# Moving the even-bank copy and the odd bank to the end of a turn in a one-core convolution kernel

## The chip, the cores and the metric

The kernel runs on one core of one Trainium2 chip. The time of a run is the device time of that core in microseconds (us). Beside the times there is the profile of one execution, in which each engine's instructions have a start and a length. The engines are TensorE (PE, matrix products), VectorE (DVE), ScalarE (ACT), GpSimd (POOL) and SyncE (SP, which starts transfers). Each works through its own queue in order and waits for others by semaphores.

## The reference

```
x: (160, 128, 32, 32) float32; U: (5, 128*128*9) float32
s1 = (max(U) - min(U)) / 3;  s2 = s1 / 5
v1 = s1 * floor(U / s1);  v2 = s2 * floor((U - v1) / s2)
w  = (v1 + v2) as (5 * 128, 128, 3, 3)
g  = group norm of x (32 groups of 4 channels, eps 1e-5)
image 5*b + n is convolved with weight set n (3 x 3, padding 1)
out = x + conv(g, w)
```

So each of the 160 images of 128 channels and 32 x 32 points is normalised, convolved with one of five quantised weight sets, and added to itself.

## The kernel before

The images are worked through in turns, `i` = 0 to 159, ordered by weight set (32 images for each). Tensors lie with the channels on the 128 partitions; an image is 1024 points in the free dimension. Products are in float16 with the operand split into a high part and a rest, so that the sum is nearly float32.

A convolution over pairs of neighbouring points is done with fewer products. For each image there are two banks of PSUM (128 x 512, float32), the even and the odd outputs. A "direct" image pairs rows: its high part `hi` goes through all nine taps (L784), its rest is combined into `rows` (L760 to L769) for L839. A "combined" image pairs columns: the differences and sums of points are made first (`v`, L674 and L704 on POOL, L686 and L693 on DVE, the last two in `combine`), then split into `vh` (ACT L734) and `vl` (DVE L740), and both go through L839. From image 7 to 29 the odd images are combined and the even ones direct.

Per image, PE, ACT and DVE work together like this:

- `begin` (PE): opens the even bank with the products of the sum quarter, 3 matmuls for a direct image, 6 for a combined one.
- `leave` (ACT L907): copies this even bank to `half` in SBUF.
- `complete` (PE): adds the products of the difference quarter to the even bank, 3 or 6 matmuls; it overwrites what `leave` reads, so it waits for it.
- `odd_from_even` (DVE L914): odd = 2 * half - even; it waits for `complete`.
- `main(i, 0)` and `main(i, 1)` (PE): the products of the even and of the odd bank, 12 matmuls each for a direct image, 6 for a combined one. `main(i, 0)` writes the even bank that L914 reads, so it waits for L914 of its image.
- `residual` (ACT L942): copies both banks to `sum`, which POOL's DMA adds to the output (L963, `accumulate`).

Nothing plans the order: the calls in `run` and `conv` are the order of each queue. The turns stand in three forms. Turn 3 (`FIRST`) has a form of its own. In turns 4 to 27, `conv(i)` gives PE `begin(i+1)`, `main(i, 0)`, `complete(i+1)`, `main(i, 1)`; ACT has `leave(i+1)` as the turn's first instruction. From turn `TWO_AHEAD` = 28 on (`steady`), `begin` runs two images ahead, `complete(i+1)` and `begin(i+2)` come ahead of the main products, and ACT's `leave(i+2)` stands behind the first statistics.

After `conv`, a turn's ACT queue has the sums for the statistics of an image some 10 to 16 turns ahead (L241), the copies of image i-1 (L942), the high part of the image two or three ahead (L734, or L636 and L644) and the squares (L248). The DVE queue has the low parts of the image two ahead (three from turn 13 on: L740, or L747 to L769) with a step of the next weight set (`later.take`, L142 to L162, L544), then L914 for image i+1, then `combine` for the image four ahead (five from turn 11 on) with another step of the weights, and for some images the statistics by DVE (L231 to L235, `BY_VECTOR`). POOL's part of `v` starts after DVE's low part of the turn (`beside_pairs`).

PSUM holds four even banks, three odd banks and a small one. SP loads two images in one DMA and stores them to the output as they are, ahead of the accumulating DMA.

Of the kernel before, what the change touches and what calls it, by code (L numbers as in the profile page):

```python
# [36 lines left out]
class Later:  # L37
# [25 lines left out]
    def finish(self):  # L63
        run(self.steps)
# [110 lines left out]
def last_of(steps, last=None):  # L175
    for last in steps:
        pass
    return last


def run(steps):

    while True:
        try:
            next(steps)
        except StopIteration as end:
            return end.value
# [134 lines left out]
def general_path(tc, keep, steps, x, u, out):  # L322
# [8 lines left out]
    with tc.If(far > 0), ExitStack() as ctx:  # L331
# [9 lines left out]
        for n in range(N_SETS):  # L341
            un = one.tile([P, C, TAPS], F32, tag="u", name=f"g_u{n}")
            nc.sync.dma_start(un, uv[n])
            wn = one.tile([P, C, TAPS], F32, tag="w", name=f"g_w{n}")
            k1, k2 = run(steps.quantise(one, un, f"g{n}", F32))
            nc.vector.tensor_scalar_mul(wn, k1, steps.s1)
            nc.vector.scalar_tensor_tensor(wn, k2, steps.s2, wn, ALU.mult, ALU.add)
# [38 lines left out]
class Main:  # L386
# [23 lines left out]

    STAT_LEAD = 15
    FURTHER = 11
    TWO_AHEAD = 28
    LOAD_LEAD = 18
    CHUNKS = 11
    STEADY = 7
# [174 lines left out]
    def keep_sums(self, n, col):  # L591
        wt = self.wts[n, col]
        run(self.both_sums(
            self.nc.gpsimd, wt[:, self.SUM], wt[:, self.DIFF], *(wt[:, k] for k in range(ROW))
        ))
# [263 lines left out]
    def steady(self, i):  # L859

        return i >= self.TWO_AHEAD

    def conv(self, i, on_the_way):


        ahead = range(i + 1, self.imgs)[:1]
        if self.steady(i) and self.steady(i - 1):
            for k in ahead:
                self.complete(k)
            for k in range(i + 2, self.imgs)[:1]:  # L870
                self.begin(k)
            self.main(i, 0, lambda: on_the_way(self.COLS[1]))
            self.main(i, 1, lambda: on_the_way(self.COLS[2]))
        elif i == self.FIRST:
            self.main(i, 0)
            self.begin(i + 1)
            on_the_way(self.COLS[1])
            self.main(i, 1)
            on_the_way(self.COLS[2])
            self.leave(i + 1)  # L880
            self.complete(i + 1)
        else:
            self.begin(i + 1)
            self.main(i, 0, lambda: on_the_way(self.COLS[1]))
            self.leave(i + 1)
            self.complete(i + 1)
            if self.steady(i):
                self.begin(i + 2)
            self.main(i, 1, lambda: on_the_way(self.COLS[2]))
        del self.v[i]  # L890

# [101 lines left out]
    def run(self):  # L993
# [54 lines left out]
        def measure(stage, *images):  # L1048
            for i in images:
                self.measure(i, (stage,))  # L1050
# [74 lines left out]
        for i in range(self.imgs):  # L1125
# [3 lines left out]
            def on_the_way(col):  # L1129
                if col == self.COLS[1]:  # L1130
                    for st in ready:
                        st.means(self.pg)
                    for *column, parts in self.columns:
                        self.turn_column(*column, parts)
                        turned.append(column)
                    self.columns.clear()
                if col == self.COLS[2]:
                    for st in middle:
                        st.variances()
# [39 lines left out]
            if i < self.FIRST:  # L1179

                if i == 0:
                    measure(0, 8, 9, 10)
                if i == 1:
                    self.normalise(4)
                    self.high_part(4)
                if i == 2:
                    self.normalise(5)
                    measure(1, 9)
                    self.high_part(5)
                    self.odd_from_even(3)  # L1190
                    self.low_part(4)
                    run(self.combinations(4))
                    measure(0, 11)
                self.residual(j)
            else:

                last = None
                for k in self.step_of(i, 2):
                    if self.combined(k):
                        last = last_of(self.low_combined(k), last)  # L1200
                    else:
                        self.low_part(k)
                        later.take(1)
                        last = last_of(self.combinations(k), last)
                last = later.take(1, last)
                if last:
                    before = self.last_but_one(last)
                    for st in scaled:
                        self.after(st.power(), before)
                    for k in self.step_of(i, 4):  # L1210
                        self.beside_pairs(k, before)
                if i > self.FIRST and self.by_hand(j):
                    self.residual(j)
                for k in by_scalar:
                    self.measure(k, (0,))
                if self.steady(i) and i + 2 < self.imgs:
                    self.leave(i + 2)
                if i > self.FIRST and not self.by_hand(j):
                    self.residual(j)
                    self.accumulate(j)  # L1220
                for st in ready:
                    if not st.late:
                        st.deviations()
                for k in self.step_of(i, 3):
                    if self.combined(k):
                        self.high_combined(k)
                        continue
                    if self.by_scalar_too(k):
                        self.normalise(k)
                    self.high_part(k)  # L1230
                for k in by_scalar:
                    self.measure(k, (1,))
# [13 lines left out]

            if i >= self.FIRST:

                if i + 1 < self.imgs:
                    self.odd_from_even(i + 1)  # L1250
                for st in scaled:
                    st.scales_by_vector()
                for k in self.step_of(i, 4):
                    if self.combined(k):
                        self.combine(k)
                    later.take(1)
                later.take_scalar()
                if b in (self.per_set - 4, self.per_set - 2):
                    later.finish()
                for st in ready:  # L1260
                    if st.late:
                        st.deviations_by_vector()
# [65 lines left out]
```

## Time and profile before

| what | value |
|---|---|
| median of 3 runs | 971.14 us (970.75 to 971.58) |
| the profiled execution | 971.98 us, its span 970.2 us |
| PE busy | 928.3 us, 96% of the span, 4432 matmuls |
| DVE busy | 858.9 us, 89% |
| ACT busy | 863.3 us, 89% |
| POOL busy | 446.0 us, 46% |
| mean granted TensorE clock | 0.993 |
| moved by DMA | 254.23 MB, mean 262 GB/s |

A row of instructions gives start, length, engine, line, operation, output from inputs, and, in brackets, how long the engine was idle before it and what ended that. A row of waits gives who waited for whom: total us, times, longest us. A matmul's length is its way through the array (0.38 us); in a row of matmuls one starts every 0.2125 us at the full clock.

### The profile page before, as it was taken

How to read it: one execution, taken by the hardware profiler on the slowest of the kernel's cores; microseconds unless marked ns; L12 is line 12 of the kernel's file. 1: busy time of each engine (PE TensorE's matmuls, PEld its weight loads, DVE VectorE, ACT ScalarE, POOL GpSimd, SP SyncE). 2: the span in 40 equal slices, each digit the busy share in tenths (PEclk: the TensorE clock that was granted, in tenths of full speed). 3: DMA queues.
4: the chain of work that ended last, by engine and by line, in shares of the span. 5: the costliest groups of instructions: out<-in, count | busy, mean ns of one | idle time of the engine just before them, and what ended most of it. 6: DMA issues, size and time to landing. Idle time of an engine off the chain costs nothing.

```text
span 970.2 us, 12948 instructions
## 1 busy us (share of the span) xinstructions
PE 928.3 (96%) x4432; PEld 434.6 (45%) x4432; DVE 858.9 (89%) x1125; ACT 863.3 (89%) x1320; POOL 446.0 (46%) x481
## 2 busy tenths in 40 slices
PE   2899979999999999999999999999999999999996
PEld 1444434444444444444444444444444444444442
DVE  7988878888899899998999899898989988889973
ACT  5779879998999999999999999999999999997660
POOL 4354433544453443454445444545444455454640
PEclk9999989999999999999999999999999999999998
DMA  9079999999999999999999999999999999756554
GB/s 353 29 270 351 329 353 330 328 326 329 321 314 317 259 283 294 276 284 269 290 252 308 286 282 284 289 277 297 263 274 266 290 280 258 162 90 102 95 93 128
DMA packets 67450, 254.23 MB, mean 262 GB/s; under 512 B 5296, under 2 KB 5296, under 8 KB 67376
## 3 DMA queue, kind: packets, MB, share of 16 engines
q1 hardware_dynamic: 45344, 173.09, 47.8%
q0 software_dynamic: 22032, 80.23, 44.1%
q8 instruction: 37, 0.61, 0.2%
q14 instruction: 37, 0.30, 0.1%
HBM read 89.19 MB, written 164.10 MB: 261 GB/s over the span
## 4 chain that ended last, share of the span: by engine, by line
PE 79%; ACT 10%; DVE 5%; issue 3%; DMA 2%; POOL 1%; SPq 0%; DVEq 0%; ACTq 0%; POOLq 0%
PE even L839 43%; PE odd L839 14%; PE even L784 11%; PE odd L784 11%; ACT junk L248 2%; ACT vh L734 2%; ACT sum L942 2%; ACT junk L241 2%; DMA u<-in_L_conv_U_dram 2%; ACT z L636 1%; ACT half L907 1%; ACT hi L644 1%; DVE ext L508 1%; DVE ext L509 1%; DVE lo L747 1%
## 5 line engine op out<-in xcount | busy, mean ns | idle before, releaser
L839 PEld LDWEIGHTS <-wt 128*128 128x128 f16 x1884 | 184.3, 99 | 211.2 <-issue 4.4
L740 DVE SCALAR_TENSOR_TENSOR vl<-v,rstd,vh 128x2048 f16<-128x2048 f32 x94 | 235.2, 2502 | 48.6 <-ACT vh L734 48.4
L839 PE MATMUL even<-vh,across 128*128 128x512 f16 x564 | 211.3, 375 | 3.5 <-ACT half L907 3.5
L839 PE MATMUL even<-vl,across 128*128 128x512 f16 x564 | 211.3, 375 | 1.7 <-DVE vl L740 1.7
L734 ACT ACTIVATE vh<-v,rstd 128x2048 f16<-128x2048 f32 x94 | 190.2, 2024 | 0.0
L784 PEld LDWEIGHTS <-wt 128*128 128x128 f16 x1242 | 121.7, 100 | 144.2 <-issue 6.6
L248 ACT ACTIVATE junk<-xt,mv 128x1024 uint8<-128x1024 f32 x152 | 176.4, 1160 | 0.3
L839 PE MATMUL even<-rows,wt 128*128 128x512 f16 x567 | 174.2, 381 | 2.5 <-ACT half L907 2.4
L963 POOL DMA_DIRECT2D out_dram<-sum x153 | 135.2, 884 | 89.7 <-ACT sum L942 74.5
L241 ACT ACTIVATE junk<-xt 128x1024 uint8<-128x1024 f32 x152 | 161.2, 1060 | 12.7 <-DMA xt<-in_x_dram 9.8
L839 PEld LDWEIGHTS <-across 128*128 128x128 f16 x1128 | 110.4, 98 | 135.5 <-issue 7.5
L784 PE MATMUL even<-hi,wt 128*128 128x496 f16 (+3 forms) x594 | 162.9, 379 | 4.8 <-DVE odd L914 3.8
L710 POOL TENSOR_SCALAR z<-xt,ngm,rstd 128x1024 f32<-128x1024 f32 x49 | 91.8, 1873 | 152.1 <-DVE rows L769 50.5
L784 PE MATMUL odd<-hi,wt 128*128 128x496 f16 (+3 forms) x594 | 161.0, 375 | 0.0
L686 DVE TENSOR_TENSOR v<-xt 128x960 f32<-128x960 f32 x94 | 155.8, 1658 | 0.5 <-POOL v L674 0.5
L907 ACT COPY half<-even 128x512 f32<-128x512 f32 x157 | 90.6, 577 | 60.1 <-PE even L839 57.1
L674 POOL TENSOR_SCALAR v<-xt,ngm 128x64 f32<-128x64 f32 x94 | 59.0, 628 | 172.8 <-DVE vl L740 74.8
L914 DVE SCALAR_TENSOR_TENSOR odd<-half,even 128x512 f32<-128x512 f32 x157 | 107.8, 687 | 17.3 <-PE even L839 13.8
L839 PE MATMUL even<-vh,wt 128*128 128x496 f16 (+1 forms) x282 | 105.6, 375 | 0.0
L839 PE MATMUL even<-vl,wt 128*128 128x496 f16 (+1 forms) x282 | 105.6, 375 | 0.0
L839 PE MATMUL odd<-vl,wt 128*128 128x496 f16 (+1 forms) x282 | 105.6, 374 | 0.0
L839 PE MATMUL odd<-vh,wt 128*128 128x496 f16 (+1 forms) x282 | 105.6, 374 | 0.0
(148 smaller groups left out, 1131.1 us busy)
## 6 DMA issues: line engine op xcount, KB each, us to landing
xt<-in_x_dram SPq DMA_DIRECT2D x78, 1024.0 KB, 9.6
out_dram<-sum POOLq DMA_DIRECT2D x153, 512.0 KB, 8.8
out_dram<-xt SPq DMA_DIRECT2D x76, 1024.0 KB, 14.2
out_dram<-xt SPq DMA_DIRECT2D x7, 512.0 KB, 6.1
u<-in_L_conv_U_dram SPq DMA_DIRECT2D x4, 576.0 KB, 14.7
xt<-in_x_dram SPq DMA_DIRECT2D x4, 512.0 KB, 9.8
range<-in_L_conv_U_dram SPq DMA_DIRECT2D x3, 576.0 KB, 8.0
u<-in_L_conv_U_dram SPq DMA_DIRECT2D x2, 288.0 KB, 3.0
```

What stands on the lines that cost most here:

```text
L241: self.nc.scalar.activation(junk, image, ACTF.Copy, scale=-1.0 / image.shape[1], accum_out=self.mv[:, j, 0:1],)
L248: self.nc.scalar.activation(junk, image, ACTF.Square, bias=self.mv[:, j, 0:1], accum_out=self.mv[:, j, 1:2],)
L674: return self.nc.gpsimd.tensor_scalar(self.view(self.v[i], 0, (512 + W // 2 - 1, 2), (W // 2, H)), self.view(self.image(i), 1, (W - 3, 2), ...
L686: nc.vector.tensor_tensor(self.view(v, 1, (511, 2), (half, H), (1, half - 1)), self.view(x, 1, (1, 2), (W, H), (2, half - 1)), self.view(x ...
L710: ins = nc.gpsimd.tensor_scalar(z, self.image(i), st.ngm[:, j], st.rstd[:, j], ALU.add, ALU.mult)
L734: self.nc.scalar.mul(vh, self.v[i], st.rstd[:, j])
L740: yield self.nc.vector.scalar_tensor_tensor(vl, self.v[i], st.rstd[:, j], self.hi[i], ALU.mult, ALU.subtract)
L784: nc.tensor.matmul(target[a][:, first:end, c0:c1], self.wts[n, col][:, k, :], tile[:, s0 : s0 + 2 * (end - first) - 1 : 2, c0 + dw : c1 + dw],
L839: self.nc.tensor.matmul(out, weights, moving, start=start and j == 0, stop=False, skip_group_check=True)
L907: self.nc.scalar.copy(half, self.eo[i][0])
L914: self.nc.vector.scalar_tensor_tensor(odd, self.half.pop(i), 2.0, even, ALU.mult, ALU.subtract)
L963: added = self.nc.gpsimd.dma_start(self.ov[n, :, b], self.sum.pop(i), accum_op=ALU.add)
```

## The change

In turns 4 up to `TWO_AHEAD`, `leave(i+1)` goes from the start of ACT's turn to behind the copies of image i-1; `complete(i+1)` goes from the middle of PE's turn to its end; and `odd_from_even(i+1)` goes behind `combine` and its step of the weights in DVE's turn. `TWO_AHEAD` becomes 20, so that turns 20 to 27 take the form of the later turns. Turn 3 and turns from 28 on keep their order. Turn 20 is the changeover, as turn 28 was.

```diff
-    TWO_AHEAD = 28
+    TWO_AHEAD = 20
...
             self.leave(i + 1)
             self.complete(i + 1)
-        else:
+        elif self.steady(i):
             self.begin(i + 1)
             self.main(i, 0, lambda: on_the_way(self.COLS[1]))
             self.leave(i + 1)
             self.complete(i + 1)
-            if self.steady(i):
-                self.begin(i + 2)
+            self.begin(i + 2)
+            self.main(i, 1, lambda: on_the_way(self.COLS[2]))
+        else:
+            self.begin(i + 1)
+            self.main(i, 0, lambda: on_the_way(self.COLS[1]))
             self.main(i, 1, lambda: on_the_way(self.COLS[2]))
         del self.v[i]
...
                 if i > self.FIRST and not self.by_hand(j):
                     self.residual(j)
                     self.accumulate(j)
+                if i > self.FIRST and not self.steady(i):
+                    self.leave(i + 1)
+                    self.complete(i + 1)
                 for st in ready:
...
-                if i + 1 < self.imgs:
+                if i + 1 < self.imgs and (i == self.FIRST or self.steady(i)):
                     self.odd_from_even(i + 1)
                 for st in scaled:
                     st.scales_by_vector()
                 for k in self.step_of(i, 4):
                     if self.combined(k):
                         self.combine(k)
                     later.take(1)
+                if i > self.FIRST and not self.steady(i):
+                    self.odd_from_even(i + 1)
                 later.take_scalar()
```

## The prediction, made before the run

> **What bounds the kernel now.** I read the busy shares first, then the waits of the stretch that the edit touches, then that stretch in order of time on TensorE (PE) and VectorE (DVE), then its granted clock.
>
> ```profile
> span 970.2 us, 12948 instructions
> PE 928.3 (96%) x4432; PEld 434.6 (45%) x4432; DVE 858.9 (89%) x1125; ACT 863.3 (89%) x1320; POOL 446.0 (46%) x481
> ```
>
> PE carries the kernel, and DVE and ScalarE (ACT) follow closely, so no engine has much room to wait. The edit touches turns 4 to 27. In the rows of PE, turn 4's first product into its own bank starts at 67.44 us, turn 20's at 175.06, turn 28's near 221. From 230 us to the end the waits of PE hold one row:
>
> ```profile
> PE even L839 <- ACT half L907: 1.6, 3, 0.6
> ```
>
> So whatever turns 4 to 27 lose or win reaches the end of the run undiminished: behind them PE has only 1.6 us in which to catch up. The waits between 56 and 230 us:
>
> ```profile
> ACT half L907 <- PE even L839: 18.0, 9, 6.9
> ...
> DVE odd L914 <- PE even L839: 12.6, 11, 3.6
> ...
> PE even L839 <- ACT half L907: 4.2, 4, 1.8
> PE even L784 <- DVE odd L914: 3.8, 3, 2.8
> ...
> PE even L839 <- DVE vl L740: 1.7, 1, 1.7
> ```
>
> The third row (PE waiting for the copy of the even bank) is what the first part of the edit can remove. The fourth row is the one to watch: PE's first product of a turn writes the even bank that DVE reads at L914 to make the odd one, so it must wait for L914. Where the largest waits stand:
>
> ```profile
> 109.76 0.38 PE L839 MATMUL even<-vh,across 128*128 128x512 f16 x1 [1.82 <-ACT half L907]
> ...
> 132.99 0.38 PE L839 MATMUL even<-vl,across 128*128 128x512 f16 x1 [1.70 <-DVE vl L740]
> 137.00 1.41 PE L784 MATMUL even<-hi,wt 128*128 128x512 f16 x3 [2.79 <-DVE odd L914]
> ```
>
> After the last of them the clock is low (stretches with the busy time of each engine, then the granted clock, DMA share and GB/s):
>
> ```profile
> 107.80:110.00 2.20, 0.38 (x3) 0.12 (x2) 2.20 (x5) 2.17 (x6) 0.23 (x1) 1.00 1.03 423
> 134.30:137.00 2.70, 0.00 (x1) 0.00 (x1) 2.70 (x7) 2.60 (x5) 0.94 (x1) 0.62 1.03 423
> 137.00:139.00 2.00, 2.00 (x5) 0.71 (x5) 2.00 (x1) 1.55 (x2) 1.23 (x2) 0.50 1.03 422
> 141.00:143.00 2.00, 2.00 (x9) 0.85 (x8) 0.00 (x0) 0.00 (x0) 1.96 (x3) 0.81 1.06 348
> ```
>
> Gaps of 1.70 and 2.79 us close together brought a clock of 0.50; the gap of 1.82 us did not. The low clock stretched twelve matmuls from 2.55 to 4.88 us (137.00 to 141.88): 2.33 us for one such spell. Last, DVE in turn 9:
>
> ```profile
> 98.65 1.28 DVE L231 BATCH_NORM_STATS2 st<-xt 128x6 f32<-128x512 f32 x2
> ...
> 100.34 2.34 DVE L740 SCALAR_TENSOR_TENSOR vl<-v,rstd,vh 128x2048 f16<-128x2048 f32 x1
> 102.60 0.61 DVE L142 SCALAR_TENSOR_TENSOR tt<-nnn,s2nhi,rest 128x384 f32<-128x384 int16 x1
> 103.13 0.68 DVE L914 SCALAR_TENSOR_TENSOR odd<-half,even 128x512 f32<-128x512 f32 x1
> 103.73 1.75 DVE L686 TENSOR_TENSOR v<-xt 128x960 f32<-128x960 f32 x1
> 105.39 0.74 DVE L693 SCALAR_TENSOR_TENSOR v<-xt,twice 128x512 f32<-128x512 f32 x1
> 106.06 0.60 DVE L143 SCALAR_TENSOR_TENSOR tt<-nnn,s2nlo,tt 128x384 f32<-128x384 int16 x1
> ```
>
> L914 for image 10 runs here before `combine` (L686, L693) and a step of the next weights (L143). The edit puts it behind them.
>
> **The change part by part.** No instruction or DMA is added or removed.
>
> (1) `leave` (L907, 0.57 us, turns 4 to 19) goes behind the two copies of image i-1, and `complete` on PE goes behind the second half of turn i's products. ACT's copy may now come up to 2.55 us (12 matmuls) or 1.27 us (6) later than before without PE waiting. So the waits of 0.45, 1.82, 1.28 and 0.69 us for L907 go; they are bounded by 0 and these 4.24 us, and I take all. Behind `leave` on ACT are queued the high part and the squares; these are needed a turn later.
>
> (2) L914 (0.70 us) now waits for `complete` at PE's turn end, and stands behind `combine`. Behind it on DVE are queued the statistics and low parts that PE's `begin` needs a turn later. PE's next turn can hide it only behind `begin` (three matmuls 0.64 us, six 1.27 us); before, half a turn of products stood between too. That cover is what goes, and what is late next is L914.
>
> (3) Turns 20 to 27 take the order that turns 28 and later have. Their waits before the edit: none on PE. The nearest row of that order, 1.6 us in 130 turns, gives 0.1 us for eight; the changeover costs between 0 and 0.6 us (its longest). I take 0.
>
> The queues of SP and POOL keep their order; the accumulating DMAs of POOL get their copies about 0.5 us earlier, and PE doesn't wait for them.
>
> For (2) I work out how long each turn becomes, from main product to main product. PE's path: 24 matmuls at 0.2125 us (5.10), or 12 (2.55) in an odd turn from 7 on, plus 0.14 to 0.3 for small statistics matmuls where the rows show them, plus `complete` 0.64 or 1.27, plus the longer of `begin` (0.64 or 1.27) and the handover to DVE and back, 1.03: 0.16 left of the last matmul, 0.12 until L914 starts (143.31 to 143.43), 0.70 for it, 0.05 until PE starts (136.95 to 137.00). DVE's path, from L914 to L914: 0.60 for L914 itself plus all between. For turn 9: 0.60 + statistics 1.69 + L740 2.27 + L142 0.53 + 0.3 until POOL's L674, which starts after L740, is done + L686 1.66 + L693 0.67 + L143 0.53 = 8.25. The others likewise from their rows; the longer path counts:
>
> ```
> turn  PE    DVE   longer before      turn  PE    DVE   longer before
>  4   6.91  5.4    6.91   6.79         12   7.70  6.5    7.70   7.33
>  5   7.01  8.4    8.40   7.02         13   4.60  8.5    8.50  10.85
>  6   7.54  4.1    7.54   7.16         14   7.40  6.0    7.40   9.35
>  7   4.46  7.2    7.20   5.20         15   4.46  3.1    4.46   4.46
>  8   7.40  4.1    7.40   7.02         16   7.40  7.5    7.50   7.02
>  9   4.60  8.25   8.25   4.59         17   4.46  4.0    4.46   4.45
> 10   7.54  4.9    7.54   9.15         18   7.54  5.5    7.54   7.16
> 11   4.46  6.75   6.75   4.45         19   4.77  3.1    4.77   5.62
> ```
>
> Sum 112.3 against 107.6 (175.06 less 67.44): +4.7 us, although the "before" column holds all the waits for L907, the gap of 4.5 us in turns 13 and 14 and the slow spell of 2.33. The loss sits in turns 5, 7, 9, 11 and 13: PE's short turns carry DVE's long ones (low part and `combine` both), and DVE then idles in the even turns.
>
> The clock comes on top. The sums leave PE idle ahead of turns 8, 10, 12 and 14 for about 2.6, 3.0, 2.3 and 2.7 us, the second and last with a further 0.5 to 1 us shortly before. These lie between the gap that kept the clock (1.82) and those that lost it (1.70 and 2.79). Bounds: none or all four slow, 0 or 9.3 us. I take two, 2 x 2.33 = 4.7, as two of the four resemble the measured pair.
>
> [...]
>
> Sum against the profiled execution's own 971.98 us: +4.7 + 4.7 = 981.4. Its time lies 0.84 above the median of the runs, so 980.5 against 971.14.
>
> **The rivals.** (a) The clock holds: +4.7, 975.8. For it: 2.3 to 2.6 us is shorter than the measured pair of gaps. Against: each gap falls in a turn whose neighbours wait too. (b) The decoupling wins. From 75.78 to 128 us the chain of waits runs almost wholly through ACT, and its copy no longer holds PE. If DVE kept up everywhere, the PE column alone would count, 98.3, or 9.4 less than before: 961.8. DVE's excess over PE in turns 5 to 13 sums to 14.0 us; below 9.4 this rival decides. Against it: the excess is made of instructions with their own rows; the only soft terms are POOL's 0.3 and L686 beside POOL (1.66 to 1.98 against 1.15 alone), at most 3 us together. (c) The excess is about two thirds of that and the clock holds: within 0.2% of before, 971.
>
> **How the numbers follow.** Forecast (one to four slow spells) 0.67, (a) 0.20, (c) 0.06, (b) 0.07. A difference below 0.2%, some 1.9 us, could not be told from none. So slower 0.87, same 0.06, faster 0.07. The range leaves out (b) and (c) and the far end: from 974.0 ((a) less 1.8 for the soft terms) to 987.0 (four spells, 971.1 + 4.7 + 9.3 = 985.1, and 1.9 for the changeover and soft terms).
>
> **What would show it.** PE's waits for L907 between 56 and 230 us should fall from 4.2 to under 1 us; those for L914 should rise from 3.8 to 12 us or more, standing ahead of turns 6, 8, 10, 12 and 14; DVE should idle before L914 in even turns (2 to 3.5 us); turn 20 should begin about 5 to 14 us later; the clock should dip one to four times between 80 and 150 us; after 230 us the waits should be as before. The prediction is wrong if DVE's L914 starts right at the end of `complete` in the odd turns 5 to 13, or if turns after 28 run faster than before.

## The result, and the profile after

The changed kernel takes 985.33 us (median of 4 runs, 983.81 to 985.85) against 970.94 us for the kernel before (970.43 to 971.58). The ratio is 1.0145, with a 95% interval of 1.0128 to 1.0163: slower by 14.4 us. The busy shares of the changed kernel, from its profile page:

```profile
span 983.9 us, 12965 instructions
PE 934.3 (95%) x4432; PEld 435.5 (44%) x4432; DVE 866.4 (88%) x1125; ACT 865.9 (88%) x1320; POOL 441.9 (45%) x481
```

The instruction counts of the five engines are those of before. Added lines shift the numbers: the copy of the even bank is now L910 (L907 before), the odd bank L917 (L914), the copies of an image L945 (L942). The waits of PE between 56 and 240 us:

```profile
PE even L784 <- DVE odd L917: 13.8, 8, 2.9
PE even L839 <- DVE odd L917: 2.4, 7, 1.1
PE small L256 <- DVE mv L234: 0.8, 1, 0.8
PE even L839 <- DVE vl L740: 0.8, 1, 0.8
PE small L256 <- DVE mv L235: 0.6, 1, 0.6
PE small L273 <- POOL dv L270: 0.6, 1, 0.6
```

The wait for ScalarE's copy (4.2 us before) is gone from the list. The wait for the odd bank went from 3.8 to 16.2 us (the first two rows). The rows of PE in order of time show where its four longest stand, ahead of turns 8, 10, 12 and 14:

```profile
99.18 0.79 PE L784 MATMUL even<-hi,wt 128*128 128x512 f16 x3 [2.47 <-DVE odd L917]
...
116.79 0.81 PE L784 MATMUL even<-hi,wt 128*128 128x512 f16 x3 [2.90 <-DVE odd L917]
...
133.35 0.80 PE L784 MATMUL even<-hi,wt 128*128 128x512 f16 x3 [2.75 <-DVE odd L917]
...
151.20 1.09 PE L784 MATMUL even<-hi,wt 128*128 128x512 f16 x3 [2.80 <-DVE odd L917]
```

Behind each of them the clock is low. The stretches of the changed kernel, with the granted clock third from the end of a row:

```profile
99.00:102.00 3.00, 2.82 (x10) 1.17 (x10) 2.61 (x5) 2.97 (x5) 0.53 (x1) 0.73 1.05 333
117.00:120.00 3.00, 3.00 (x10) 1.15 (x9) 2.97 (x7) 1.99 (x3) 0.00 (x0) 0.57 1.08 355
135.00:138.00 3.00, 3.00 (x12) 1.63 (x11) 2.72 (x6) 2.97 (x4) 1.47 (x2) 0.51 1.07 299
153.00:156.00 3.00, 3.00 (x11) 1.17 (x10) 2.01 (x4) 2.34 (x5) 2.09 (x3) 0.67 1.03 422
```

On VectorE in turn 9, `combine` (L686, L693) and the step of the weights (L143) now stand ahead of the odd bank:

```profile
107.51 0.69 DVE L917 SCALAR_TENSOR_TENSOR odd<-half,even 128x512 f32<-128x512 f32 x1 [4.50 <-PE even L839]
108.12 1.28 DVE L231 BATCH_NORM_STATS2 st<-xt 128x6 f32<-128x512 f32 x2
...
109.80 2.34 DVE L740 SCALAR_TENSOR_TENSOR vl<-v,rstd,vh 128x2048 f16<-128x2048 f32 x1
112.06 0.61 DVE L142 SCALAR_TENSOR_TENSOR tt<-nnn,s2nhi,rest 128x384 f32<-128x384 int16 x1
112.96 1.98 DVE L686 TENSOR_TENSOR v<-xt 128x960 f32<-128x960 f32 x1 [0.28 <-POOL v L674]
114.86 0.74 DVE L693 SCALAR_TENSOR_TENSOR v<-xt,twice 128x512 f32<-128x512 f32 x1
115.52 0.61 DVE L143 SCALAR_TENSOR_TENSOR tt<-nnn,s2nlo,tt 128x384 f32<-128x384 int16 x1
116.05 0.68 DVE L917 SCALAR_TENSOR_TENSOR odd<-half,even 128x512 f32<-128x512 f32 x1
```

VectorE first idles 4.50 us until PE's turn 8 ends (turn 8 ran at the low clock), and then needs 8.54 us to the next odd bank, with one pause of 0.28 us, while PE, with 4.6 us of work in turn 9, waits for it. So one engine waits in the even turn and the other in the odd one.

The starts of the odd-bank instruction give a clock for the turns. The table, worked out from the rows of VectorE, has the time from the odd bank of image i to that of image i+1, for both kernels and the first five experiments:

```
turn   before   after   e1      e2      e3      e4      e5
 5      5.63     8.86    6.78    9.04    5.62    8.88    8.23
 6      7.78     7.53    7.78    4.97    7.78    7.52    7.52
 7      5.72     7.24    4.34    7.24    5.47    7.24    7.23
 8      6.50     9.06    7.65    4.84    6.50    7.38    7.39
 9      5.42     8.54    5.56    8.54    5.42    8.55    6.86
10      8.18     9.20    7.78    5.81    8.18    7.51    7.52
11      5.25     7.37    4.21    8.42    5.26    7.37    7.37
12      7.53     9.35    7.94    7.13    7.54    7.69    9.35
13     12.17     8.49   10.22    8.60   12.14    8.49    6.81
14      7.17     9.08    9.07    8.18    7.05    8.17    8.17
15      5.85     4.21    5.87    3.46    5.85    4.21    4.20
16      5.63     8.54    7.39    8.79    5.63    8.54    8.54
17      6.32     4.21    6.27    4.01    6.30    4.19    4.19
18      5.29     7.78    7.53    7.59    5.31    7.78    7.78
19      6.14     4.51    5.88    3.72    6.14    4.51    4.51
```

The odd bank of image 20 comes at 172.66 us before and at 188.79 after; a part of these 16.13 us is its new place within the turn. PE's first main product of turn 20 starts at 189.79 us in place of 175.06, 14.73 later, and that of turn 30 14.72 later (250.15 against 235.43). The odd bank of image 50 comes 14.71 us later than before, and that of image 159 14.70 us later: behind turn 30 nothing is caught up.

### The profile page after: what moved, and what is told of

Same layout as the page of the kernel before. It is cut to its first block, busy times and chain, and to the rows that moved or that the text cites. A ratio compares the mean times of both kernels' runs of the same rounds, so it can differ in the third digit from the quotient of the medians.

```text
span 983.9 us, 12965 instructions
## 1 busy us (share of the span) xinstructions
PE 934.3 (95%) x4432; PEld 435.5 (44%) x4432; DVE 866.4 (88%) x1125; ACT 865.9 (88%) x1320; POOL 441.9 (45%) x481
## 4 chain that ended last, share of the span: by engine, by line
PE 81%; DVE 7%; issue 4%; ACT 3%; DMA 2%; POOL 1%; SPq 1%; DVEq 0%; POOLq 0%; ACTq 0%
PE even L839 43%; PE odd L839 14%; PE even L784 12%; PE odd L784 11%; DMA out_dram<-xt 2%; ACT vh L734 1%; DMA range<-in_L_conv_U_dram 1%; ACT sum L945 1%; ACT junk L248 1%; DVE vl L740 1%; DVE odd L917 1%; DVE lo L747 1%; DVE tt L144 1%; DVE tt L143 0%; DVE st L231 0%
## 5 line engine op out<-in xcount | busy, mean ns | idle before, releaser
L784 PE MATMUL even<-hi,wt 128*128 128x496 f16 (+3 forms) x594 | 165.7, 384 | 14.6 <-DVE odd L917 13.8
L686 DVE TENSOR_TENSOR v<-xt 128x960 f32<-128x960 f32 x94 | 160.9, 1712 | 1.9 <-POOL v L674 1.9
L710 POOL TENSOR_SCALAR z<-xt,ngm,rstd 128x1024 f32<-128x1024 f32 x49 | 87.3, 1781 | 157.4 <-DVE rows L769 50.1
L674 POOL TENSOR_SCALAR v<-xt,ngm 128x64 f32<-128x64 f32 x94 | 60.9, 648 | 188.7 <-DVE vl L740 90.7
L910 ACT COPY half<-even 128x512 f32<-128x512 f32 x157 | 90.6, 577 | 57.8 <-PE even L839 54.5
L917 DVE SCALAR_TENSOR_TENSOR odd<-half,even 128x512 f32<-128x512 f32 x157 | 108.2, 689 | 24.0 <-PE even L839 16.8
```

The costliest lines, as they stand in the source:

```text
L674: return self.nc.gpsimd.tensor_scalar(self.view(self.v[i], 0, (512 + W // 2 - 1, 2), (W // 2, H)), self.view(self.image(i), 1, (W - 3, 2), ...
L686: nc.vector.tensor_tensor(self.view(v, 1, (511, 2), (half, H), (1, half - 1)), self.view(x, 1, (1, 2), (W, H), (2, half - 1)), self.view(x ...
L710: ins = nc.gpsimd.tensor_scalar(z, self.image(i), st.ngm[:, j], st.rstd[:, j], ALU.add, ALU.mult)
L784: nc.tensor.matmul(target[a][:, first:end, c0:c1], self.wts[n, col][:, k, :], tile[:, s0 : s0 + 2 * (end - first) - 1 : 2, c0 + dw : c1 + dw],
L910: self.nc.scalar.copy(half, self.eo[i][0])
L917: self.nc.vector.scalar_tensor_tensor(odd, self.half.pop(i), 2.0, even, ALU.mult, ALU.subtract)
```

## The experiments

The theory to test (A): the late `complete` lets VectorE's turn begin only when PE's ends, and the late odd bank makes PE's next turn wait for all of VectorE's; both together tie the two engines turn by turn, and the clock loss comes on top. The rivals: the late `complete` alone (B), VectorE's order alone (C), the low clock as a mere sign (D), ScalarE's late copies (E).

**e1: the odd bank at its old place, the rest as changed.**

```diff
-                if i + 1 < self.imgs and (i == self.FIRST or self.steady(i)):
+                if i + 1 < self.imgs:
                     self.odd_from_even(i + 1)
...
-                if i > self.FIRST and not self.steady(i):
-                    self.odd_from_even(i + 1)
```

> The changed kernel, but the odd bank is made at its old place, ahead of `combine`; the copy and `complete` stay late. Theory A (VectorE's combine ahead of the odd bank, in turns where PE has little to do): turns 5, 7, 9 and 11 fall back to PE's own 4.5 to 7 us, but from turn 13 on the low part and `combine` of neighbouring turns now meet in the short turns 15, 17 and 19 (+1.4, +1.9, +0.6 us), and turn 13 keeps its pile: 973 to 978 us. Rival B (a late `complete` alone is what costs, whatever stands ahead of the odd bank): 982 to 986 us.

Measured: 976.97 us, ratio to before 1.0055 (1.0039 to 1.0072). B is out; A's figure holds, and so do its turns in the table: 7, 9 and 11 fall back to 4.2 to 5.6 us, while 15, 17 and 19 take 5.9 to 6.3 in place of 4.2 to 4.5, because from turn 13 on the low part and `combine` of neighbouring turns fall together in PE's short turns. So neither of the two places of the odd bank suits both stretches.

**e2: only the odd bank moved, on the kernel before.**

```diff
+                moved = self.FIRST < i < 20
-                if i + 1 < self.imgs:
+                if i + 1 < self.imgs and not moved:
                     self.odd_from_even(i + 1)
...
+                if moved:
+                    self.odd_from_even(i + 1)
                 later.take_scalar()
```

> The kernel before, with only the odd bank moved behind `combine` in turns 4 to 19; copy, `complete` and the changeover stay as before. Theory A in its full form (late `complete` and late odd bank cost only together, because VectorE's turn can then begin only when PE's ends): VectorE gets its start in the middle of PE's turn and has half a turn more, so about the time of before, 969 to 974 us. Rival C (VectorE's order alone costs): 980 to 986 us.

Measured: 971.94 us, ratio 1.0002 (0.9993 to 1.0012): no difference, which excludes C. VectorE's long turns are as long as in the changed kernel (turn 9: 8.54 us in both), but here the next turn is short (turn 10: 5.81 against 9.20 us), since `complete` comes in the middle of PE's turn and VectorE can go on at once. The rows of VectorE in e2 show it:

```profile
107.57 0.68 DVE L914 SCALAR_TENSOR_TENSOR odd<-half,even 128x512 f32<-128x512 f32 x1
...
113.38 0.68 DVE L914 SCALAR_TENSOR_TENSOR odd<-half,even 128x512 f32<-128x512 f32 x1
```

Neither of the two carries a wait. In the changed kernel the odd bank that ends turn 10 waited 3.31 us for PE:

```profile
125.25 0.70 DVE L917 SCALAR_TENSOR_TENSOR odd<-half,even 128x512 f32<-128x512 f32 x1 [3.31 <-PE even L839]
```

e1 and e2 together: one move costs about 5 us, the other nothing, both 14. The loss is in the combination.

**e3: only the earlier changeover, on the kernel before.**

```diff
-    TWO_AHEAD = 28
+    TWO_AHEAD = 20
```

> The kernel before with TWO_AHEAD = 20 and nothing else. Both theories: 970 to 972 us, PE waits between 180 and 240 us under 0.7 us. If the earlier changeover has a share in the loss, 973 us or more.

Measured: 972.02 us, ratio 1.0003 (0.9994 to 1.0013). On the kernel before, this part of the edit has no share.

**e4: the changed kernel with PE kept busy.** The repeated products start the bank anew and overwrite the first set.

```diff
-    def begin(self, i):
+    def begin(self, i, times=1):
...
-        for step in self.KS:
-            self.product(even, i, 2, step, self.SUM, start=step == self.KS[0])
+        for _ in range(times):
+            for step in self.KS:
+                self.product(even, i, 2, step, self.SUM, start=step == self.KS[0])
...
-            self.begin(i + 1)
+            self.begin(i + 1, 2 if i in (8, 10, 12, 14) else 1)
```

> The changed kernel; in turns 8, 10, 12 and 14 the `begin` products of the next image are done twice (6 matmuls more each, 1.27 us, the first set overwritten), so that PE is idle about 1.3 us less ahead of its wait for the odd bank. Theory A with the clock as a term of its own (four spells of 1.67 us): no dip of the clock between 80 and 160 us, 977 to 980 us, although 24 matmuls are added. Rival D (the low clock is only a sign: VectorE sets the pace of these turns anyway): 984 to 987 us.

Measured: 980.39 us, ratio 1.009 (1.0073 to 1.0107), against 1.0145 for the changed kernel: 0.4 us above what theory A had expected, and clear of rival D. The turns that had the low clock, in e4:

```profile
99.00:102.00 3.00, 3.00 (x15) 1.38 (x15) 2.38 (x4) 2.97 (x5) 0.76 (x1) 1.00 1.07 328
117.00:120.00 3.00, 3.00 (x17) 1.58 (x16) 2.96 (x5) 1.51 (x6) 1.54 (x2) 1.00 1.05 276
132.00:135.00 3.00, 3.00 (x16) 1.40 (x15) 2.72 (x5) 2.97 (x6) 2.07 (x3) 1.00 1.06 273
150.00:153.00 3.00, 3.00 (x15) 1.34 (x14) 2.97 (x5) 0.81 (x2) 2.76 (x4) 1.00 1.08 322
```

The clock is full although 24 matmuls were added, and PE waits for the odd bank as before, only shorter (1.21 to 1.63 us). In the table, turns 8, 10 and 12 lose 1.66 to 1.69 us each and turn 14 0.91, together 5.9 us; in turn 14 VectorE's own 8.17 us is the floor that then shows, and PE waits 1.00 us for the odd bank behind it. D is out: the low clock is a cost of its own.

**e5: the changed kernel with less work on VectorE and more on ScalarE.**

```diff
-    BY_VECTOR = (8, 10, 11, 14, 19, 24, 29, 34)
+    BY_VECTOR = (8, 10, 11, 29, 34)
```

> The changed kernel, with the statistics of images 14, 19 and 24 by ScalarE: about 1.69 us less on VectorE in each of turns 5, 9 and 13, and 2.4 us more on ScalarE for each. Theory A: turns 5 and 9 and 13 get shorter by 1.2 to 1.7 us each and one or two of the four low-clock spells (1.67 us) go: 976 to 981 us. Rival E (ScalarE, whose copies stand late, sets the pace): 986 us or more.

Measured: 978.6 us, ratio 1.0084 (1.0068 to 1.0099). Turns 9 and 13 got shorter by 1.68 us each, just the statistics that were taken from VectorE; turn 5 only by 0.63, less than expected. ScalarE's added work (872.4 us busy against 865.9) cost nothing that can be seen, so E is out. Three of the four low-clock spells went, more than expected, and one of them without a shorter gap: between 60 and 240 us the clock is 1.00 but for 120 to 140 us, where it is 0.91. PE's row ahead of turn 8 in e5, and the stretch that holds it:

```profile
99.44 0.79 PE L784 MATMUL even<-hi,wt 128*128 128x512 f16 x3 [2.47 <-DVE odd L917]
```

```profile
99.00:102.00 3.00, 2.56 (x13) 1.18 (x13) 2.88 (x5) 3.00 (x3) 0.27 (x1) 1.00 1.05 351
```

The gap is 2.47 us, exactly as long as the one that lost the clock in the changed kernel. What the traces show of the two is in the last section.

**e6: the kernel before with PE kept busy in turn 14.** The edit of `begin` is that of e4; in `conv`:

```diff
-            self.begin(i + 1)
+            self.begin(i + 1, 3 if i == 14 else 1)
             self.main(i, 0, lambda: on_the_way(self.COLS[1]))
             self.leave(i + 1)
```

> The kernel before; in turn 14 the `begin` products of image 15 are done three times (12 matmuls more), which fill 2.5 of the 2.8 us in which PE waits for the odd bank. If the low clock behind that wait costs its 2.3 us: 968 to 969.3 us and no dip at 135 to 142 us. If the turns behind it absorb it: 970.5 to 971.5 us.

Measured: 969.76 us, ratio 0.9983 (0.9974 to 0.9992), 1.5 us below the median of before beside it (971.25), with 12 matmuls more: between the two expectations, nearer to the first. In turn 14 the time from odd bank to odd bank falls from 7.17 to 4.84 us, and the stretch behind the wait has the full clock. From the odd bank of image 3 to that of image 159 the profiled execution is 2.2 us shorter than that of before; why the medians show only 1.5 is left open. The stretch:

```profile
137.00:139.00 2.00, 1.74 (x9) 0.78 (x8) 2.00 (x2) 1.88 (x4) 1.57 (x2) 1.00 1.04 426
```

**e7: the kernel before with other statistics on VectorE.**

```diff
-    BY_VECTOR = (8, 10, 11, 14, 19, 24, 29, 34)
+    BY_VECTOR = (8, 10, 11, 14, 19, 22, 29, 34)
```

> The kernel before, with the statistics of image 22 by VectorE in place of image 24's: the 1.7 us go from the pile of turns 12 and 13 to turn 10, where VectorE waits 1.5 us for the high part. If VectorE's pile sets the gap before turn 14: the gap falls from 2.8 to about 1.1 us and the low clock goes, 966.5 to 969 us. If ScalarE, with 2.4 us more in turn 12, takes its place: 970 to 974 us.

Measured: 969.89 us, ratio 0.9988 (0.9979 to 0.9997), above what the first theory expected and below the second. The gap did not go, it moved. Ahead of turn 14 PE no longer waits for the odd bank; in turn 13 it waits for ScalarE. PE in e7, in order of time:

```profile
130.82 1.44 PE L839 MATMUL even<-rows,wt 128*128 128x512 f16 x3 [3.52 <-ACT half L907]
```

ScalarE, with one image's statistics more in turn 12, is late with its copy in turn 13, and the low clock follows there (0.50 from 131 to 136 us). So before turn 14 VectorE's pile sets the gap, but ScalarE's comes right behind it.

**e8: the changed kernel with the late order up to turn 27.**

```diff
-    TWO_AHEAD = 20
+    TWO_AHEAD = 28
```

> The changed kernel with TWO_AHEAD = 28, so that turns 20 to 27 have the late order too. Theory A: in these turns VectorE's long work falls into PE's long turns, so only the handover (0.4 us) and the slower `combine` beside GpSimd in four turns count, +1.6 to +3.6 us on the changed kernel: 986.5 to 989 us. If each pair of turns lost what the pairs of turns 5 to 12 lost, 995 us or more.

Measured: 993.57 us, ratio 1.0231 (1.0215 to 1.0246), 8.2 us above the changed kernel: more than theory A had expected, and less than the 995 us of a loss in each pair of turns. From main product to main product, turns 25, 27 and 28 took 2.1, 2.9 and 2.5 us more than in the changed kernel; the other turns of 20 to 29 took 1.4 us more together. The estimate had missed these three. From image 30 on the combined images are no longer the odd ones. In turn 27, with a combined image and little work for PE, VectorE makes the low part of image 30 and the `combine` of image 32, both combined; in turn 25 it makes the low part of image 28 and the `combine` of image 30. Turn 28 is now the changeover. The longest wait of PE stands right behind turn 27:

```profile
244.97 0.80 PE L784 MATMUL even<-hi,wt 128*128 128x512 f16 x3 [3.39 <-DVE odd L917]
```

From odd bank to odd bank turn 27 took 8.02 us and turn 25 6.67, against the 4.5 us of PE's path. So in these two the mechanism is that of turns 5 to 13, and the list of the turns that have it was incomplete. Why the changeover costs more at turn 28 than at turn 20 was not tested.

**e9: e6, and ScalarE's copy of a weight column earlier.** In the turns in which a weight column is turned, `keep_taps` goes from behind the squares to behind the copies of image i-1.

```diff
                     self.accumulate(j)
+                for n_of, col in turned:
+                    self.keep_taps(n_of, col)
                 for st in ready:
...
             for n_of, col in turned:
-                self.keep_taps(n_of, col)
+                if i < self.FIRST:
+                    self.keep_taps(n_of, col)
```

> The kernel before with the repeated `begin` of turn 14 (as in e6) and, in the turns in which a weight column is turned, ScalarE's copy of it (`keep_taps`) right behind the copies of image i-1 in place of behind the squares. VectorE's statistics at 128.37 us waited 1.26 us for that copy; if VectorE's pile in turns 12 and 13 sets the gap before turn 14, that wait goes, and the time is 1 to 1.3 us below e6: 967.5 to 968.7 us. If ScalarE's later high part takes its place: 969.5 us or more.

Measured: 971.37 us, ratio 0.9996 (0.9987 to 1.0005). The first expectation missed it. The number of the second fits, and its cause, a later high part of ScalarE, shows in a later turn. VectorE's wait in turn 12 is gone and turn 13 took 10.82 us against 12.14 in e6, but turn 21 took 1.8 us longer than in e6, turn 22 0.4 us less, and turns 27 to 29 together 0.7 us more. So the edit wins where VectorE waits for this copy and loses some 2 us in later turns, where it doesn't. In turn 20 the copy stands ahead of ScalarE's high part, which starts at 171.10 us against 170.55 in e6; GpSimd's L674 then starts at 177.91 us against 176.53, VectorE waits 0.89 us for it, and its L686 takes 1.97 us in place of 1.15. The cause of the 0.7 us in turns 27 to 29 is open. In the profiled execution the odd bank of image 3 also came 1.3 us later than in e6, and no edit touches what stands ahead of it; this start varies from 58.0 to 59.6 us over the runs, and why is left open.

**e10: the same in turn 12 alone.**

```diff
                     self.accumulate(j)
+                for n_of, col in turned:
+                    if i == 12:
+                        self.keep_taps(n_of, col)
                 for st in ready:
...
             for n_of, col in turned:
-                self.keep_taps(n_of, col)
+                if i != 12:
+                    self.keep_taps(n_of, col)
```

> As e9, but ScalarE's early copy of the weight column in turn 12 alone. In e9 turn 13 got 1.3 us shorter, as the theory of VectorE's pile has it, and the turns 21, 28 and 29 lost 3 us behind the same edit. If these are separate, this gives e6's gain and 1.2 us more: a ratio to before of 0.996 to 0.998, 967.5 to 969 us. If turn 13's gain is given back later: as e6, 0.998 to 0.999.

Measured: 968.4 us, ratio 0.9967 (0.9955 to 0.998), as expected, and faster than both kernels (the 3 us that the expectation names were counted too high: 2.1, as said above). VectorE in e10 no longer waits between `combine` and the statistics (1.26 us before), so that the odd bank of image 14 comes at 134.96 us in place of 136.26. The rows of before, then those of e10:

```profile
128.37 0.16 DVE L296 TENSOR_SCALAR twice<-small 128x4 f32<-128x4 f32 x1 [1.26 <-ACT wt L564]
...
136.26 0.69 DVE L914 SCALAR_TENSOR_TENSOR odd<-half,even 128x512 f32<-128x512 f32 x1
```

```profile
126.42 0.74 DVE L693 SCALAR_TENSOR_TENSOR v<-xt,twice 128x512 f32<-128x512 f32 x1
127.08 0.15 DVE L296 TENSOR_SCALAR twice<-small 128x4 f32<-128x4 f32 x1
...
134.96 0.69 DVE L915 SCALAR_TENSOR_TENSOR odd<-half,even 128x512 f32<-128x512 f32 x1
```

## Why the prediction was right, and what was mis-sized

The direction and the mechanism held: 985.33 us lies inside the range of 974 to 987, 4.8 us above the figure of 980.5. Two terms of the sum were too small. The upper end of the range was made up of four spells at 2.33 us and 1.9 us for the changeover and the soft terms; it was other terms that filled it, a cheaper clock and longer turns.

- The turns. The table summed turns 4 to 19 to 112.3 us at the full clock. In the trace they take 122.0 us from main product to main product (67.79 to 189.79 us), 9.7 more. Of these, 5.9 us are the low clock, by e4. The other 3.8 us (measured length less the sum's, in turn 14 that of e4's row) are: turn 4 +0.87, turn 5 +0.45, turn 9 +0.28, turn 11 +0.60, turn 14 +0.8, turn 16 +0.80. In turn 4 0.60 us of it is a wait that the prediction had not named: with `complete` gone from the middle of the turn, PE reaches the statistics matmul L273 before GpSimd has its input. In turn 11 VectorE waited 0.93 us for GpSimd's `rstd`, ahead of `combine`. In turn 14 the sum had 6.0 us for VectorE, and e4 shows 8.17, more than PE's 7.40; among it are a wait of 0.95 us for GpSimd's `rstd` and 0.96 us for L310 (0.16 before). In turns 5, 9 and 16 it is `combine` itself: L686 took 1.98 to 2.00 us, behind a wait of 0.28 to 0.49 us for GpSimd's L674, where the sum had 1.66 in turn 9. It now follows the low part so closely that it starts while GpSimd still works on the same tile.
- The clock. The sum took two spells of 2.33 us, 4.7 together: too few and too dear. There were four, behind which turns 8, 10, 12 and 14 are 1.67 to 1.69 us longer than the sum's. e4 takes the spells away: turns 8, 10 and 12 get that much shorter and turn 14 0.91, 5.9 together, so they cost by themselves. That 4.7 came near 5.9 is in part luck, since the two errors run against each other. The choice of two rested on the length of the gaps: those of 2.47 to 2.90 us all lost the clock in the changed kernel, and e5 shows that the length alone doesn't decide.

Added up: 4.7 from the sum, 3.8 and 5.9 are 14.4 us for turns 4 to 19; turn 4 began 0.35 us later, which makes 14.7 from image 50 on. The span grew by 13.7 only, because the end behind the last odd bank took 14.8 us in place of 15.8; over the runs that end varies from 14.8 to 16.2 us, and why is left open.

The steps in detail. (1) PE's waits for ScalarE's copy went from 4.2 us to none, as taken. (2) The odd bank is what came late in its place, ahead of turns 6, 8, 10, 12 and 14, and VectorE idled 2.2 to 4.5 us ahead of it in turns 6, 8, 10 and 12; e1 and e2 show that it takes both moves. The prediction gave the price as a property of the late odd bank together with the lost cover, and never priced the moves apart. (3) The changeover costs nothing on the kernel before (e3), and in the changed kernel PE's delay is the same at turn 20 (14.73 us) as at turn 30 (14.72). Rival (a), a clock that holds, gave +4.7 us; e4, in which the clock does hold, stands 8.6 us above its kernel before (980.39 against 971.75): about the 4.7 and the 3.8 of the turns. Rival (b), ScalarE's relief, failed where the prediction put it: the relief is real, but the wait is for VectorE.

## What to carry to other kernels

When two engines alternate in work, look at the turn, not at the shares: VectorE had 11% to spare here and PE 4%, and tying them twice per turn made each turn as long as the longer of the two. Before moving a step to the end of a turn, list for every kind of turn what then stands between one hand-over and the next on both engines, and check the turns in which the pattern changes. And where PE must wait anyway, a few repeated products in the gap can be worth more than they cost (4.9 us in e4, 1.5 in e6).

## What was not expected of the hardware

- A gap of PE of the same length, 2.47 us, was followed by the low clock in the changed kernel and by the full clock in e5; gaps of 2.05, 2.10 (e5) and 2.23 us (e2) kept it, gaps of 2.74 (e5), 2.75 to 2.90 (the changed kernel) and 2.80 us (e2) lost it, and behind the gap of 3.39 us in e8 the matmuls start 0.21 us apart, at the full clock.
- The profiles of the two kernels record when the granted clock changed. The four spells of the changed kernel begin at 100.37, 117.44, 134.51 and 151.57 us, each 17.07 us behind the one before, and last 3.41 us each at a clock of 0.50; the one spell of the kernel before in these turns lasts 6.83 us, 134.94 to 141.77. In the 3.41 us ahead of a spell PE was busy for 1.19, 0.65, 1.16 and 0.61 us in the changed kernel, and for 1.21 us in the kernel before. In e5 the one low spell between 60 and 240 us begins near 129.0 us (the clock is 0.84 from 127 to 130 us and 0.59 from 130 to 133). Counted back from there in steps of 3.41 us, the gap of 2.47 us falls across two steps, in which PE was busy for 2.04 and 2.32 us. So these rows differ in PE's busy time where the gaps are equally long; what decides about the clock was not shown, since no run set a gap to test it. The rows of the changed kernel, then of e5:

```profile
96.96:100.37 3.41, 1.19 (x6) 0.58 (x6) 3.38 (x6) 2.82 (x3) 0.06 (x1) 1.00 1.06 422
100.37:103.79 3.42, 3.42 (x10) 1.17 (x8) 1.67 (x5) 2.81 (x6) 1.95 (x2) 0.50 1.04 268
```

```profile
94.93:98.35 3.42, 2.04 (x10) 0.84 (x9) 3.14 (x5) 3.42 (x8) 2.22 (x3) 1.00 1.03 339
98.35:101.76 3.41, 2.32 (x11) 1.07 (x11) 3.38 (x6) 3.41 (x4) 0.03 (x1) 1.00 1.05 365
101.76:105.17 3.41, 3.41 (x17) 1.57 (x16) 0.55 (x3) 3.38 (x8) 1.93 (x2) 1.00 1.04 312
```

- These lengths also give an estimate of the price. A spell of 3.41 us at half the clock costs half of it, 1.71 us, if PE has work throughout; 1.66 to 1.69 us were measured in turns 8, 10 and 12. Before, the spell behind the double gap lasted 6.83 us, and PE stood idle until 137.00; half of the other 4.77 us is 2.4, and 2.33 us were measured.
- In the kernel before, L686 took 1.15 us alone (at 144.37 us) and 1.98 us where it started beside GpSimd's subtraction (L704, 1.03 us) on the same tile (at 78.89 us).
